# Four-layer graph network on one core: layer 1's own-feature half of the last 12 node tiles moved beside the stage's first gathers

## The chip, the cores and the metric

The kernel runs on one core of one Trainium2 chip. The metric is the device time of one execution in microseconds; of several executions the median is given. A core has a matrix engine (PE, with its weight loads listed apart as PEld), a vector engine (DVE), an activation engine (ACT), a general engine (POOL) and a queue engine for transfers (SP). Each executes its own list of instructions in order, and semaphores tie them together. SBUF is the working memory (128 partitions), PSUM holds the matrix engine's results in 8 banks. Transfers run on 16 DMA engines shared by all queues.

## The reference, cut to what matters

There are 6250 nodes with 256 features and 100000 edges sorted by their target `dst`, whose density falls towards high node numbers. Rows are normalised and rectified, and four graph layers follow; the result is added to x.

```python
def _sage_mean(h, src, dst, n, deg, W_self, W_neigh, b):
    msum = jax.ops.segment_sum(h[src], dst, num_segments=n)
    h_neigh = msum / jnp.clip(deg, 1.0)[:, None]
    return h @ W_self + h_neigh @ W_neigh + b
...
h = _sage_mean(features, edge_src, edge_dst, n, deg, W1_self, W1_neigh, b1)
h = _sage_pool(h, edge_src, edge_dst, n, deg, W2_pool, b2_pool, W2_self, W2_neigh, b2)
h = _sage_gcn(h, edge_src, edge_dst, n, deg, W3_neigh, b3)
h = _sage_mean(h, edge_src, edge_dst, n, deg, W4_self, W4_neigh, b4)
return h @ W_fc + b_fc
```

`_sage_pool` applies relu(h @ W_pool + b_pool) to every node before it takes the maximum over the sources of a node's edges. The change lies in layer 1, whose output is used only through products that the kernel has folded together: W1_self @ W2_pool (`Wa`), W1_neigh @ W2_pool (`Wb`) and one bias row (`crow`). So layer 1 computes for every node the row relu(h0 Wa + mean Wb + crow), where h0 are the node's own normalised features and mean is the mean over its sources.

## The kernel before, in words

The nodes are cut into 49 tiles of 128 (`NT` = 49). The first 8 (`H1`) are hub tiles with very many edges; their sums are computed as dense products with count matrices, which the kernel builds on the way. The other 41 are tail tiles, whose edges are gathered row by row.

A first stage, until about 105 us, normalises the rows. It keeps the result as three bf16 parts side by side in SBUF (`Z1`, 3 x 256 columns a tile, whose sum is the fp32 value), writes the same to the table `tab_h`, and computes `Wa`, `Wb` and `crow`.

Layer 1's main loop is the helper `sums` (lines 460 to 543). It runs over 474 steps, one for every 128 edges of the tail. In each step POOL gathers 128 source rows into one of 14 slots of `ring` (L483), DVE makes a one-hot matrix of the targets (L479), and PE multiplies it with the three parts of the rows (L505) into a PSUM bank. After four steps DVE adds that bank into the accumulators of the tiles that it touches (L532, L534). Each step then advances three lists of side work: the hub's builds and dense products (L337 to L351 and L564), spread evenly over all but the last 24 steps; `todo`, the tiles that are being finished, at most two at a time; and `aside`, a list of generators of which the first is advanced by one `yield` a step until it is exhausted, then the next. Before, `aside` holds `tail_checks` (small tests of the sorted order on DVE) and `segments` (loads and small DVE work for layer 2). What is left in `aside` and `todo` after the last step is run off behind it.

A tile is finished by the generator `done1` (lines 1094 to 1132): degree and scale on DVE, the mean `m1` on ACT (L1103); then, three steps later, PE turns the tile's own features (L1111: six bf16 products with the identity, three parts for each of two halves, which sum the parts in PSUM) and its mean (L1114) into the bank `pt`; ACT copies both halves into `th` (L1116), which SP stores in `tab_t` for layer 2 (L1117). Four steps later PE multiplies the own half with `Wa` (L1124, four instructions since a 512-column fp32 product with 128 rows appears as two) and, a step after that, the mean's half with `Wb` (L1127) into the bank `pm`. DVE adds `crow` (L1130), ACT rectifies (L1131), SP stores the row tile in `tab_p` (L1132, shown as rows). The pools `pst1` and `psm1`, which hold `pt` and `pm`, have one bank each, so two tiles can't hold them at once. Tail tiles finish in the order of their numbers, hub tiles between them as their dense products end.

Layer 2 begins with gathers from `tab_p` (L1475), which may touch any row, so the first of them needs the row stores of all tiles.

The order on each engine is set at build time by the framework: an instruction whose inputs are ready by its estimate can be placed before one that stands earlier in the program. DVE's order in the first stage is fixed by hand. Semaphores are placed by the framework.

Of the kernel before, what the change touches and what calls it, by code (L numbers as in the profile page):

```python
# [9 lines left out]
F32 = mybir.dt.float32  # L10
# [10 lines left out]
P = 128  # L21
# [56 lines left out]
def fast_path(  # L78
# [15 lines left out]
    nc = tc.nc  # L94
    N, FI = x.shape
    E = src.shape[0]
    FH = W1_self.shape[1]
    FO = W_fc.shape[1]
    NT = (N + P - 1) // P
# [5 lines left out]
    KI = FI // P  # L105
# [42 lines left out]
    for w0, w1_ in ((0, NW1), (NW1, NW)):  # L148
        for k in range(k_of[w0]):
            n = sum(1 for w in range(w0, w1_) if k_of[w] > k)  # L150
# [12 lines left out]
    tab_t = dram.tile([NT, P, FH], F32, name="tab_t")  # L163
# [42 lines left out]
    ident_b = const.tile([P, P], BF16, name="ident_b")  # L206
# [41 lines left out]
    def bank(pool, tag, name, shape=None, bufs=None):  # L248
        t = pool.tile([P, FH], F32, tag=one_tag.get(id(pool), tag), name=name, **({"bufs": bufs} if bufs else {}))
        if shape is None:  # L250
            return t
        n = math.prod(shape)
        if len(shape) == 1:
            return t[:, :n]
        return t[:, :n].rearrange("p (a b) -> p a b", b=shape[1])
# [340 lines left out]
    def segments():  # L596
        dstI, dstF, eqf = scratch(T, I32), scratch(T), scratch(T)
        flen, fhalf = (ahead.tile([P, 1], F32, name=n) for n in ("flenf", "fhalf"))
        flenI = ahead.tile([P, 1], I32, name="flenI")
        for b, tb in enumerate(BLOCKS):  # L600
            t0 = offs[b] // P
            for flat, put in ((sflat, srcI), (dflat, dstI)):
                tc.keep_in_program_order(nc.sync.dma_start(
                    put[:, t0 : t0 + tb],
                    flat[offs[b] : offs[b + 1]].rearrange("(p t) -> p t", t=tb),
                ))
        for _ in range(60):
            yield 1
        nc.vector.tensor_copy(dstF, dstI)
        nc.vector.tensor_tensor(same[:, 1:], dstF[:, 1:], dstF[:, : T - 1], op=ALU.is_equal)  # L610
        yield 1
        for b, tb in enumerate(BLOCKS):
            t0 = offs[b] // P
            sl_ = slice(t0, t0 + tb)
            nc.vector.memset(same[:, t0 : t0 + 1], 0.0)
            nc.vector.tensor_copy(rows_df[:, b : b + 1], dstF[:, t0 : t0 + 1])
            nc.vector.tensor_copy(rows_dl[:, b : b + 1], dstF[:, t0 + tb - 1 : t0 + tb])
            nc.vector.tensor_scalar(eqf[:, sl_], dstF[:, sl_], rows_df[:, b : b + 1], None,
                                    op0=ALU.is_equal)
            nc.vector.tensor_reduce(flen, eqf[:, sl_], AX.X, ALU.add)  # L620
            nc.vector.tensor_scalar(flen, flen, -1.0, None, op0=ALU.add)
            kept_row(b, flen, flenI, fhalf)
            nc.vector.tensor_scalar(flen, flen, float(P), float(run_at[b]), op0=ALU.mult,
                                    op1=ALU.add)
            nc.vector.tensor_add(fixI[:, b : b + 1], flen, pidx)
            yield 1
# [4 lines left out]
    Z1 = zpool.tile([P, NT, 3 * FI + 4], BF16, name="Z1")  # L631
# [6 lines left out]
    Wa = w1pool.tile([P, KI, FH], F32, name="Wa")  # L638
    Wb = w1pool.tile([P, KI, FH], F32, name="Wb")
    crow = w1pool.tile([P, FH], F32, name="crow")  # L640
# [12 lines left out]
    with ExitStack() as pro:  # L653
        pst = pro.enter_context(tc.tile_pool(name="pst0", bufs=3, space=PSUM))
# [299 lines left out]
        def tail_checks(pool):  # L954
            wrong = pool.tile([P, JR, P], BF16, name="wrongf", bufs=1)
            for c in range(JR):
                nc.vector.tensor_tensor(wrong[:, c, :], rD[:, c, :], rN[:, c, :], op=ALU.is_gt)
                yield 1
            nc.vector.tensor_reduce(bad[:, 0:1], wrong, AX.XY, ALU.max)
            yield 1  # L960
            far = wrong[:, : JR - JC, :]
            for c in range(JR - JC):
                nc.vector.tensor_tensor(
                    far[:, c, :].rearrange("p (g k) -> p g k", k=G),
                    d3[:, c, :].rearrange("p (g k) -> p g k", k=G),
                    dB[:, c * P // G : (c + 1) * P // G, None].to_broadcast([P, P // G, G]),
                    op=ALU.subtract,
                )
                yield 1
            nc.vector.tensor_scalar(dT, dT, float(NP), None, op0=ALU.is_lt)  # L970
            yield 1
            lo = g_of[H1][0] * G - JC * P
            for c in range(JR - JC):
                nc.vector.scalar_tensor_tensor(far[:, c, :], far[:, c, :], float(P), d3[:, c, :],
                                               op0=ALU.is_ge, op1=ALU.mult)
                yield 1
            nc.vector.tensor_reduce(bad[:, 2:3], far.rearrange("p c e -> p (c e)")[:, lo:],
                                    AX.X, ALU.max)
            yield 1
# [104 lines left out]
    with ExitStack() as on:  # L1084
        pst = on.enter_context(tc.tile_pool(name="pst1", bufs=1, space=PSUM))
        psm = on.enter_context(tc.tile_pool(name="psm1", bufs=1, space=PSUM))
        psg = on.enter_context(tc.tile_pool(name="psg1", bufs=2, space=PSUM))
        psd = on.enter_context(tc.tile_pool(name="psd1", bufs=2, space=PSUM))
        wk = on.enter_context(tc.tile_pool(name="fl1", bufs=2))

        def h0_row(s):
            return Z1[:, s, :]

        def done1(d, acc):
            r = rmean[:, d : d + 1]
            nc.vector.tensor_copy(deg[:, d : d + 1], acc[:, FI : FI + 1])
            nc.vector.tensor_scalar_max(r, acc[:, FI : FI + 1], 1.0)
            nc.vector.reciprocal(r, r)
            o = only[:, d : d + 1]
            nc.vector.tensor_scalar(o, acc[:, FI + 1 : FI + 2], float(P), None, op0=ALU.mult)  # L1100
            nc.vector.tensor_add(o, o, acc[:, FI + 2 : FI + 3])
            m1 = wk.tile([P, FI], F32, name="m1")
            nc.scalar.activation(m1, acc[:, :FI], AF.Copy, scale=r)  # L1103
            yield 1
            yield 1
            yield 1
            pt = bank(pst, "pt", "pt_m", (2 * KI, P))
            for k in range(KI):
                for part in range(3):
                    c = part * FI + k * P  # L1110
                    nc.tensor.matmul(pt[:, k, :], Z1[:, d, c : c + P], ident_b,  # L1111
                                     start=(part == 0), stop=(part == 2))
            for k in range(KI):
                nc.tensor.transpose(pt[:, KI + k, :], m1[:, k * P : (k + 1) * P], ident)  # L1114
            th = wk.tile([P, 2 * KI, P], F32, name="th")
            nc.scalar.copy(th, pt)  # L1116
            nc.sync.dma_start(tab_t[d].rearrange("p (k n) -> p k n", n=P), th)  # L1117
            yield 1
            yield 1
            yield 1  # L1120
            yield 1
            ph = bank(psm, "pm", "pm_hp")
            for k in range(KI):
                nc.tensor.matmul(ph, th[:, k, :], Wa[:, k, :], start=(k == 0), stop=False)  # L1124
            yield 1
            for k in range(KI):
                nc.tensor.matmul(ph, th[:, KI + k, :], Wb[:, k, :], start=False,  # L1127
                                 stop=(k == KI - 1))
            hp = wk.tile([P, FH], F32, name="hpf")
            nc.vector.tensor_add(hp, ph, crow)  # L1130
            nc.scalar.activation(hp, hp, AF.Relu)  # L1131
            nc.sync.dma_start(tab_p[d * P : (d + 1) * P, :], hp)  # L1132

        todo = []
        As.append(wk.tile([P, NT, P], F8, name="A1", bufs=1))
        builds = [None] + [build(d, As[d % 2], (sk1, mk1, 0), bpool, psb1) for d in range(1, H1)]
        denses = [dense(range(NT), lambda s, A=As[d % 2]: A[:, s, :], h0_row, FI, psd,
                        lambda acc, d=d: todo.append(done1(d, acc)), extra=3)
                  for d in range(H1)]
        work = []  # L1140
        for d in range(H1):
            work += merged(denses[d], builds[d + 1]) if d + 1 < H1 else denses[d]
        hub = Hub(made.rest() + work)
        sums(wk, psg, tab_h, FI, srcT, keyT, JC * P, H1, done1, 14, hub, counts=3, todo=todo, rest=24,
             aside=[tail_checks(wk), segments()])
    layer1.close()


# [1166 lines left out]
```

## Time and profile before

| | us |
|---|---|
| median of 3 runs | 2751.69 |
| lowest, highest | 2750.1, 2760.69 |
| profiled execution, time | 2753.24 |
| profiled execution, span from first to last instruction | 2751.4 |

| engine | busy us in the span | share |
|---|---|---|
| PE (matrix products) | 2372.0 | 86% |
| PEld (weight loads, beside PE) | 1281.9 | 47% |
| DVE | 2071.6 | 75% |
| ACT | 906.2 | 33% |
| POOL | 1942.6 | 71% |

All times in the views are microseconds from the first instruction. Layer 1's gathers run from 104.9 to 712.7 us, layer 2's from 738.3 to 1833.9 us. A share over the whole span mixes stages with different limits, so the views below are taken stretch by stretch. A group's row names line, engine, operation, what is written and read, shape and count, then busy time and mean duration in ns, then the idle time of its engine right before it and what ended that. A matrix product's duration is its latency; in a dense run they overlap, and the step from one start to the next is shorter (the 128x512 fp32 products of L1124 last 592 ns each, and a block of four takes 1.72 us in the chain). The granted clock is the share of full speed that PE was allowed.

### The profile page before, as it was taken

How to read it: one execution, taken by the hardware profiler on the slowest of the kernel's cores; microseconds unless marked ns; L12 is line 12 of the kernel's file. 1: busy time of each engine (PE TensorE's matmuls, PEld its weight loads, DVE VectorE, ACT ScalarE, POOL GpSimd, SP SyncE). 2: the span in 40 equal slices, each digit the busy share in tenths (PEclk: the TensorE clock that was granted, in tenths of full speed). 3: DMA queues.
4: the chain of work that ended last, by engine and by line, in shares of the span. 5: the costliest groups of instructions: out<-in, count | busy, mean ns of one | idle time of the engine just before them, and what ended most of it. 6: DMA issues, size and time to landing. Idle time of an engine off the chain costs nothing.

```text
span 2751.4 us, 39155 instructions
## 1 busy us (share of the span) xinstructions
PE 2372.0 (86%) x11540; PEld 1281.9 (47%) x11671; DVE 2071.6 (75%) x5542; ACT 906.2 (33%) x2177; POOL 1942.6 (71%) x2267
## 2 busy tenths in 40 slices
PE   3578999999887666798899969976999999999998
PEld 2245666776553322343344424432444444565554
DVE  8888777765599898789889988862667776466665
ACT  5467777763278786321311111110000101000000
POOL 6477777776467776777777777744777776677775
PEclk9799999999898787899999989998999999999999
DMA  9566777777699999999999999978999998888886
GB/s 286 154 170 192 208 211 217 229 220 211 207 362 356 328 360 340 364 352 350 327 358 356 359 340 340 343 251 313 373 380 389 387 368 303 259 239 241 240 243 198
DMA packets 350747, 806.43 MB, mean 293 GB/s; under 512 B 56014, under 2 KB 147638, under 8 KB 350492
## 3 DMA queue, kind: packets, MB, share of 16 engines
q0 software_dynamic: 146160, 514.05, 56.8%
q1 hardware_dynamic: 137784, 207.04, 20.7%
q10 hardware_dynamic: 66580, 82.73, 9.0%
q8 instruction: 94, 1.54, 0.2%
q14 instruction: 129, 1.06, 0.1%
HBM read 605.25 MB, written 199.17 MB: 292 GB/s over the span
## 4 chain that ended last, share of the span: by engine, by line
PE 32%; DMA 27%; DVE 8%; issue 5%; POOL 3%; ACT 0%; ACTq 0%; SPq 0%; DVEq 0%; POOLq 0%
DMA X<-rows,srcIf 12%; PE pd L564 11%; PE pg L505 6%; PE pd L556 4%; DMA rows<-X 3%; DVE run L1456 3%; DMA ring<-tab_r,srcE 3%; DMA ring<-tab_s,srcE 3%; DVE X L1456 2%; PE pd L557 2%; POOL X L1475 2%; PE pg L500 2%; PE pm_prf L1383 2%; DMA zt<-tab_r 2%; PE pm_prf L1377 1%
## 5 line engine op out<-in xcount | busy, mean ns | idle before, releaser
L1475 POOL DMA_INDIRECT X<-rows,srcIf x782 | 744.1, 952 | 276.4 <-issue 148.2
L1456 DVE SCALAR_TENSOR_TENSOR run<-run,samef,X 128x512 f32<-128x512 f32 x758 | 571.4, 754 | 45.3 <-DMA X<-rows,srcIf 41.4
L505 PE MATMUL pg<-ring,hot 128*128 128x259 bf16 (+1 forms) x2432 | 516.0, 322 | 68.4 <-DMA ring<-tab_h,srcT 39.5
L483 POOL DMA_INDIRECT ring<-tab_h,srcT x474 | 455.6, 961 | 157.6 <-issue 58.5
L534 DVE SCALAR_TENSOR_TENSOR acc<-pg,M,acc 128x256 f32<-128x256 f32 (+2 forms) x694 | 356.8, 539 | 116.0 <-PE pg L505 83.8
L483 POOL DMA_INDIRECT ring<-tab_r,srcE x342 | 333.7, 976 | 132.0 <-issue 59.4
L564 PE MATMUL pd<-r,ae 128*128 128x512 bf16 x1493 | 367.6, 384 | 37.2 <-DVE acc L1241 35.1
L483 POOL DMA_INDIRECT ring<-tab_s,srcE x314 | 299.8, 955 | 116.5 <-PE pg L501 35.2
L505 PEld LDWEIGHTS <-hot 128*128 128x128 bf16 x2448 | 240.3, 99 | 278.7 <-issue 120.1
L1456 DVE SCALAR_TENSOR_TENSOR X<-X,samef,run 128x512 f32<-128x512 f32 x379 | 281.4, 743 | 48.8 <-issue 17.8
L556 PE MATMUL pd<-zt,ac 128*128 128x512 bf16 x835 | 290.0, 380 | 7.4 <-DMA ac<-tab_a 5.8
L564 PEld LDWEIGHTS <-ae 128*128 128x128 fp8e4 x1536 | 151.2, 99 | 252.0 <-issue 107.0
L557 PE MATMUL pd<-zt,ac 128*128 128x256 bf16 x882 | 241.1, 273 | 2.7 <-DVE zt L312 0.2
L479 DVE TENSOR_SCALAR hot<-iota_bf,keyE 128x128 bf16<-128x128 bf16 x656 | 159.8, 268 | 106.6 <-PE pg L505 76.4
L564 PE MATMUL pd<-zt,ac 128*128 128x512 bf16 x797 | 221.2, 379 | 0.9
L1383 PE MATMUL pm_prf<-unf,hTf 128*128 128x512 f32 x392 | 191.3, 616 | 3.0 <-ACT hTf L1373 3.0
L338 ACT ACTIVATE hs<-ht,onef 128x128 bf16<-128x128 bf16 x396 | 153.8, 393 | 107.5 <-PE pb L346 106.4
L564 PE MATMUL pd<-Z,A 128*128 128x256 bf16 (+1 forms) x1176 | 184.3, 273 | 0.4 <-ACT A L351 0.3
L479 DVE TENSOR_SCALAR hot<-iota_bf,keyT 128x128 bf16<-128x128 bf16 x474 | 126.8, 276 | 53.8 <-PE pg L505 52.2
L346 PE MATMUL pb<-hm,hs 128*128 128x392 bf16 x461 | 147.9, 345 | 13.8 <-DVE hm L340 13.3
L337 ACT ACTIVATE ht<-iota_bf,sk 128x128 bf16<-128x128 bf16 x396 | 153.1, 398 | 8.4
L1391 ACT CAST r<-pm_prf 128x512 bf16<-128x512 f32 x49 | 28.7, 585 | 376.2 <-PE pm_prf L1383 303.3
(347 smaller groups left out, 3597.9 us busy)
## 6 DMA issues: line engine op xcount, KB each, us to landing
rows<-X SPq DMA_DIRECT2D x385, 256.0 KB
tab_r<-r ACTq DMA_DIRECT2D x49, 384.0 KB
tab_t<-th SPq DMA_DIRECT2D x49, 256.0 KB
rows<-hpf SPq DMA_DIRECT2D x49, 256.0 KB
th<-tab_t ACTq DMA_DIRECT2D x49, 256.0 KB
X<-rows,srcIf POOLq DMA_INDIRECT x782, 5.7
ac<-tab_a ACTq DMA_DIRECT2D x90, 112.0 KB
tab_h<-Z SPq DMA_DIRECT2D x16, 579.0 KB
```

What stands on the lines that cost most here:

```text
L337: nc.scalar.activation(t, iota_b, AF.Abs, bias=sk[:, r : r + 1])
L338: nc.scalar.activation(hots[0], t, AF.Relu, bias=one, scale=-1.0)
L479: nc.vector.tensor_scalar(hot[j], iota_b, keyT[:, j - jb : j - jb + 1], None, op0=ALU.is_equal)
L483: nc.gpsimd.indirect_dma_start(out=ring[:, j % deep, :], out_offset=None, in_=table, in_offset=bass.IndirectOffsetOnAxis(ap=srcT[:, j - jb ...
L505: nc.tensor.matmul(pg[:, : F + c], hot[j], X[:, part * F : (part + 1) * F + c], start=(k == 0 and part == 2), stop=(k == n - 1 and part == 1),
L534: nc.vector.scalar_tensor_tensor(acc[d], half, m, acc[d], op0=ALU.mult, op1=ALU.add)
L556: nc.tensor.matmul(hold[0], a, z[:, : 2 * F], start=(s == ss[0]), stop=False)
L557: nc.tensor.matmul(hold[0][:, :F], a, z[:, 2 * F :], start=False, stop=(s == ss[-1]))
L564: nc.tensor.matmul(hold[0][:, : F + c], a, z[:, part * F : (part + 1) * F + c], start=(s == ss[0] and part == 2 and s != own), stop=(s == ...
L1383: nc.tensor.matmul(pm, hT[:, c, :], un[:, c, :], start=False, stop=(c == KH - 1))
L1456: nc.vector.scalar_tensor_tensor(put, held, st, row, op0=ALU.mult, op1=ALU.max)
L1475: nc.gpsimd.indirect_dma_start(out=X[:, k, :], out_offset=None, in_=tab_p, in_offset=bass.IndirectOffsetOnAxis(ap=srcI[:, t : t + 1], axis=0),
```

## The change

A new generator, `own_ahead`, stands first in `aside`. For the tiles 37 to 48 (`AHEAD` = 49 - 12 to the end) it does the half of the finish that needs only the tile's own features: the six products with the identity, a copy to SBUF (`tho`, one buffer), the store of the first half of `tab_t[d]`, the product with `Wa`, and the addition of `crow` into a tile `own{d}` of its own, which stays in SBUF (12 x 2 KB a partition). It uses the same banks `pt` and `pm` as `done1`. It yields six times a tile. For those tiles `done1` leaves out the six products and the product with `Wa`, copies and stores only the second half, starts its product with `Wb` afresh, and adds `own{d}` where it added `crow`. The first 37 tiles are finished as before.

```diff
+        AHEAD = NT - 12
+        own1 = {}
+
+        def own_ahead():
+            for d in range(AHEAD, NT):
+                pt = bank(pst, "pt", "pt_o", (2 * KI, P))
+                for k in range(KI):
+                    for part in range(3):
+                        c = part * FI + k * P
+                        nc.tensor.matmul(pt[:, k, :], Z1[:, d, c : c + P], ident_b,
+                                         start=(part == 0), stop=(part == 2))
+                t = wk.tile([P, KI, P], F32, name="tho", bufs=1)
+                nc.scalar.copy(t, pt[:, :KI, :])
+                nc.sync.dma_start(tab_t[d][:, : KI * P].rearrange("p (k n) -> p k n", n=P), t)
+                yield 1
+                yield 1
+                ph = bank(psm, "pm", "pm_o")
+                for k in range(KI):
+                    nc.tensor.matmul(ph, t[:, k, :], Wa[:, k, :], start=(k == 0),
+                                     stop=(k == KI - 1))
+                    yield 1
+                own1[d] = wk.tile([P, FH], F32, name=f"own{d}", bufs=1)
+                nc.vector.tensor_add(own1[d], ph, crow)
+                yield 1
+                yield 1
+
         def done1(d, acc):
...
             pt = bank(pst, "pt", "pt_m", (2 * KI, P))
-            for k in range(KI):
-                for part in range(3):
-                    c = part * FI + k * P
-                    nc.tensor.matmul(pt[:, k, :], Z1[:, d, c : c + P], ident_b,
-                                     start=(part == 0), stop=(part == 2))
+            h0 = KI if d >= AHEAD else 0
+            if not h0:
+                for k in range(KI):
+                    for part in range(3):
+                        c = part * FI + k * P
+                        nc.tensor.matmul(pt[:, k, :], Z1[:, d, c : c + P], ident_b,
+                                         start=(part == 0), stop=(part == 2))
...
-            nc.scalar.copy(th, pt)
-            nc.sync.dma_start(tab_t[d].rearrange("p (k n) -> p k n", n=P), th)
+            nc.scalar.copy(th[:, h0:, :], pt[:, h0:, :])
+            nc.sync.dma_start(tab_t[d][:, h0 * P :].rearrange("p (k n) -> p k n", n=P),
+                              th[:, h0:, :])
...
-            for k in range(KI):
-                nc.tensor.matmul(ph, th[:, k, :], Wa[:, k, :], start=(k == 0), stop=False)
+            if not h0:
+                for k in range(KI):
+                    nc.tensor.matmul(ph, th[:, k, :], Wa[:, k, :], start=(k == 0), stop=False)
...
-                nc.tensor.matmul(ph, th[:, KI + k, :], Wb[:, k, :], start=False,
+                nc.tensor.matmul(ph, th[:, KI + k, :], Wb[:, k, :], start=bool(h0 and k == 0),
                                  stop=(k == KI - 1))
...
-            nc.vector.tensor_add(hp, ph, crow)
+            nc.vector.tensor_add(hp, ph, own1[d] if h0 else crow)
...
         sums(wk, psg, tab_h, FI, srcT, keyT, JC * P, H1, done1, 14, hub, counts=3, todo=todo, rest=24,
-             aside=[tail_checks(wk), segments()])
+             aside=[own_ahead(), tail_checks(wk), segments()])
```

## The prediction

> **What bounds the kernel now.** The change touches layer 1 alone, so I read the engines' busy time by stretch first. Columns: stretch, its length, then busy us and instruction count of PE, PEld, DVE, ACT, POOL, then granted clock, DMA share, GB/s.
>
> ```profile
> 105.00:200.00 95.00, 69.93 (x362) 40.19 (x363) 79.82 (x367) 51.93 (x138) 73.06 (x73) 0.83 0.62 172
> 200.00:300.00 100.00, 86.50 (x570) 58.09 (x569) 74.93 (x343) 71.38 (x207) 75.93 (x80) 0.98 0.69 202
> 300.00:450.00 150.00, 145.11 (x1016) 103.39 (x1016) 112.41 (x419) 111.64 (x304) 113.74 (x120) 1.00 0.71 209
> 450.00:600.00 150.00, 150.00 (x1028) 105.64 (x1026) 110.19 (x406) 103.58 (x277) 113.44 (x121) 1.00 0.74 218
> 600.00:720.00 120.00, 119.89 (x809) 83.00 (x807) 67.08 (x260) 46.76 (x107) 79.38 (x84) 1.00 0.70 210
> ```
>
> PE has slack early (25.1 us idle up to 200, 13.5 us up to 300) and none from 450 on. POOL does about 120 instructions per 150 us, one per 1.25 us, from 200 to 600, then only 84 in 120 us. So I looked at the 474 gathers of L483 over the whole stage, then in two stretches, the second with what ended POOL's idle time there.
>
> ```profile
> L483 POOL DMA_INDIRECT ring<-tab_h,srcT x474: 941/947/1407, 104.9 to 712.7; - x158
> DMA to landing us min/median/max: 3.0/3.5/6.3
> ...
> L483 POOL DMA_INDIRECT ring<-tab_h,srcT x177: 942/947/1061, 400.0 to 621.1; - x177
> ...
> L483 POOL DMA_INDIRECT ring<-tab_h,srcT x66: 941/946/1014, 622.3 to 712.7; - x66
> ...
>   PE pg L505: 15.3, 21
> ```
>
> Between 400.0 and 621.1, 177 gathers have 176 steps of 1.256 us: that is POOL's own pace (947 ns each, the rest the gap before the next). Between 622.3 and 712.7 the 65 steps take 90.4 us; at 1.254 us they would take 81.5. **8.9 us are lost**, and PE's L505 ended 15.3 us of the idle: a gather overwrites the ring slot of 14 gathers before, and PE is late in freeing it. Before 600 POOL sets the pace, after it PE does. What PE does there, in the stretch 616 to 735, by group (busy, mean ns, idle before):
>
> ```profile
> L505 PE MATMUL pg<-ring,hot 128*128 128x256 bf16 (+1 forms) x246 | 38.0, 273 | 0.0
> L564 PE MATMUL pd<-Z,A 128*128 128x256 bf16 (+1 forms) x255 | 36.7, 273 | 0.1
> L1127 PE MATMUL pm_hp<-Wb,th 128*128 128x512 f32 x59 | 27.8, 592 | 0.0
> L1124 PE MATMUL pm_hp<-Wa,th 128*128 128x512 f32 x56 | 26.6, 597 | 0.9 <-ACT th L1116 0.7 <-DVE hpf L1130 0.2
> L1111 PE MATMUL pt_m<-ident_b,Z 128*128 128x128 bf16 x84 | 7.0, 219 | 0.0
> ```
>
> The last view is the chain that ended last, here from the last ring product to layer 2's first gather (start us, length, what), with two earlier pieces for the price of one tile, and one row of L505 for when the ring products end:
>
> ```profile
> 663.99 1.72 PE pm_hp L1124 x4
> 665.71 0.34 PE pt_m L1111 x6
> ...
> 724.64 0.70 DVE hpf L1130
> 725.38 1.98 PE pm_hp L1124 x4
> 727.37 1.72 PE pm_hp L1127 x4
> 729.38 0.59 ACT th L1116
> 730.02 1.98 PE pm_hp L1124 x4
> 732.00 1.73 PE pm_hp L1127 x4
> 733.82 0.70 DVE hpf L1130
> 734.54 0.64 ACT hpf L1131
> 735.20 2.01 DMA rows<-hpf
> 737.85 0.41 issue
> 738.26 1.07 POOL X L1475
> ```
>
> ```profile
> L505 PE MATMUL pg<-ring,hot x234: 271/273/275, 622.4 to 724.6; 128*128 128x256 bf16 x78, 128*128 128x259 bf16 x39
> ```
>
> The last gather starts at 712.7, but its products end only at 724.6, 11.9 us later, where a landing of 3.5 us would allow about 5: PE carries some 7 us of backlog. Then the last two tiles run one behind the other through the single bank pm, and layer 2's first gather follows the last row store by about a microsecond. Layer 2 starts when layer 1 ends, so time won here is won in the whole.
>
> **The change, part by part.** *Removed from the late part.* Which tiles fall there is told by the ACT rows of L1103, which begin a tile's finish:
>
> ```profile
> L1103 ACT ACTIVATE m<-acc,rmeanf x12: 492/508/509, 609.6 to 726.5; 128x256 f32<-128x256 f32 x12
> ```
>
> Twelve tail tiles begin their finish from 609.6 on: exactly tiles 37 to 48. Each loses six L1111 (0.34 us) and four L1124 (1.72 us) on PE, 2.06 us by the two chain pieces; twelve are **24.7 us**, all from a stretch where PE has under 3 us idle. (The groups hold 14 tiles, 56 and 84 instructions: two are hub tiles, which keep theirs.) The copy L1116 is halved; DVE's L1130 stays.
>
> What that is worth has a floor, POOL's pace. Less PE work of 24.7 us against a backlog and loss of 7 + 8.9 = 16 us means PE is no longer the limit: the 65 steps run at 1.254 us and the last gather starts at 622.3 + 81.5 = 703.8. PE can follow: from 622 to 724.6 it is busy all 102.3 us; ten of the removed tiles' work, 20.6 us, lies in it (the Wa of the last two lies behind, the first transposes before); 102.3 - 20.6 = 81.7 us of work against 81.5 us of gathers. It is just enough, and the two or three microseconds by which it might not be are eaten by the slack of the last 24 gathers, in which the hub has ended. The last products then end about 5 us after the last gather (3.5 landing, 0.95 issue, six products), at 708.8 instead of 724.6: **15.8 us**.
>
> *The tail.* From 724.64 to 738.26 are 13.6 us. Two L1124 blocks of 1.98 us go, and half the copy of 0.59 us. The nearest row for a half copy is this one, 0.37 us:
>
> ```profile
> L276 ACT COPY B4f<-pm_w x8: 372/372/377, 752.9 to 779.5; 128x256 f32<-128x256 f32 x8
> ```
>
> 13.6 - 3.96 - 0.2 = 9.4 us: **4.2 us** less. For tile 48 alone acc, m1, transposes, copy and one L1127 block come to the same, so no other wait takes its place. Sum of gains: 15.8 + 4.2 = 20.0 us.
>
> *Added early.* own_ahead advances one step per gather, six steps a tile, so 72 gathers or 90 us: 105 to about 195. Per tile six transposing products, a half copy on ACT, a store on SP, four Wa products, and one DVE add of 128x512 as in L1130 (0.70 us in the chain). PE gets 24.7 us at full clock; the early Wa blocks are slower, and PE's waits there are these (105 to 200):
>
> ```profile
> L505 PE MATMUL pg<-ring,hot 128*128 128x256 bf16 (+1 forms) x210 | 44.8, 312 | 25.1 <-DMA ring<-tab_h,srcT 22.1 <-DVE acc L534 1.3 <-DVE hm L340 0.9
> ...
> L1124 PE MATMUL pm_hp<-Wa,th 128*128 128x512 f32 x8 | 4.9, 696 | 0.0
> ...
> L338 ACT ACTIVATE hs<-ht,onef 128x128 bf16<-128x128 bf16 x60 | 23.5, 393 | 21.9 <-PE pb L346 21.7
> ```
>
> At 696/592 the price is 29 us, against 25.1 us idle, of which 22.1 wait for gathers that POOL hasn't brought: the cover. What is left, 4 us, makes PE late but not POOL: 14 slots less the three in flight are 11 gathers or 13.8 us of reserve, and 200 to 300 has 13.5 us idle to win it back. If the cover were gone, all 29 us would count, since POOL has no slack anywhere. DVE gets 8.4 us and has 15.2 us free in 95; tail_checks, which stood first, moves behind. ACT gets 4.5 us, with 43 us free. SP gets twelve more stores; behind them wait the loads of srcI and the hub's stores, needed only after layer 1. The new wait is PE's Wa block on the ACT copy; behind it stand L505 and L346, and then POOL by way of the ring, DVE by way of acc.
>
> POOL already loses early: 73 instructions in 95 us are 3 short of 76, 3.8 us. I take as much again for the added traffic, 3.5 us; bounds are -4 us (PE busier at a higher clock, that loss gone) and +29.
>
> The Trainium skill, "TensorE: Matmul & The Clock Gate", Part 1, says that the PE clock halves after an idle window of about 3.4 us and returns after as much sustained work. The granted 0.83 early against 1.00 late agrees. By it the filled gaps would lift the clock for the old products too, and the early loss would be nil: 3.5 us better than my sum.
>
> **Sum.** 20.0 - 3.5 = 16.5 us. The profiled execution took 2753.24 us with a span of 2751.4; 2753.2 - 16.5 = 2736.7. The median of the runs, 2751.69, is 1.6 lower: **2735**.
>
> **The rivals.** *PE blocks early (slower).* Each Wa block waits on a copy that stands on ACT behind L338, which itself waits for PE: 21.7 us in 60 there. If that costs PE w per tile, POOL stalls by 29 + 12w - 25.1 - 13.8 us and the change loses once this passes 20: w = 2.5 us. At w = 4 us the stall is 38 us: 2751.7 + 38 - 20 = 2770. Against it: two gathers (2.5 us) lie between copy and product, and ACT is idle 45% of that stretch.
>
> *Only the tail wins.* If late PE busy hides waits for the gathers, removing work there frees nothing and only 4.2 us of the tail remain: 2747. Against: L505's idle there is 0.0, and the gathers wait for PE.
>
> *Given back in layer 2.* 25 KB more per partition stay held to the end of layer 1, and layer 2's first loads (bases of its constants and weights) are placed anew; if they come late by half the gain, 2743. For: layer 2's stretches are orders of waits too; against: its first gather waits for nothing but the row store.
>
> **Chances.** Forecast 0.62 (2729 to 2742), tail only 0.08, given back 0.19, blocked early 0.11. What a measurement can tell from no change is 0.5%, 13.8 us, thus 2738. Of the forecast 0.52 lies under that, with 0.02 of the third case: faster 0.54; blocked early gives slower 0.10; the rest, 0.36, within. The range runs from 2728 (early loss turned to a gain) to 2752, which takes in tail and given back and leaves out most of the blocked case.
>
> **What would show it.** Right: POOL's gather steps after 622 at 1.25 us, last start near 704 to 708, L505's last under 6 us after it, layer 2's first gather at 718 to 724; PE's idle up to 200 nearly gone, POOL's 73 instructions up to 200 down by three at most. Wrong: gather steps over 1.35 us between 105 and 300 with PE as releaser, Wa blocks of the new lines idle on ACT by over 2 us each, or layer 2's gathers taking longer than the 1095.6 us that they span now:
>
> ```profile
> L1475 POOL DMA_INDIRECT X<-rows,srcIf x782: 940/946/1437, 738.3 to 1833.9; - x196
> ```

## The result and the profile after

The changed kernel took 2730.28 us (median of five runs, 2726.8 to 2738.27); the kernel before, run beside it, 2751.52 (five runs, 2748.9 to 2760.69). The ratio is 0.9921, its 95% interval 0.99 to 0.9941: 16 to 28 us faster. The profiled execution took 2726.8 us with a span of 2725.0.

In the lines of the changed kernel the generator's products are L1112 (`Wa` times own features), its copy L1106 and its addition L1116; in `done1` the own transposes are L1139 (before L1111), the mean's L1142, the copy L1144, `Wa` L1154, `Wb` L1157, the addition of `crow` or `own` L1160 (before L1130), the activation L1161. Layer 2's gather is L1505. L483, L505, L534 and L564 have kept their numbers.

First the stretches of layer 1 after the change (stretch, length; busy us and count of PE, PEld, DVE, ACT, POOL; granted clock, DMA share, GB/s):

```profile
105.00:200.00 95.00, 81.09 (x469) 47.27 (x468) 80.28 (x347) 55.83 (x154) 72.44 (x75) 0.96 0.65 180
...
450.00:600.00 150.00, 150.00 (x1028) 105.51 (x1027) 108.63 (x405) 103.49 (x276) 113.61 (x119) 1.00 0.74 218
600.00:720.00 120.00, 110.32 (x732) 77.20 (x730) 69.49 (x280) 46.45 (x110) 78.82 (x83) 0.98 0.72 217
```

Early, PE's idle time went from 25.1 to 13.9 us and its clock from 0.83 to 0.96, while POOL issued 75 instructions instead of 73. Late, PE has 9.7 us idle where it had none. Next the gathers of the late part, with what ended POOL's idle time, then the rows of the ring products and of layer 2's gathers:

```profile
L483 POOL DMA_INDIRECT ring<-tab_h,srcT x67: 942/946/1051, 620.2 to 702.9; - x67
...
  PE pg L505: 6.4, 21
```

```profile
L505 PE MATMUL pg<-ring,hot x273: 270/273/417, 599.9 to 710.1; 128*128 128x256 bf16 x91, 128*128 128x259 bf16 x46
```

```profile
L1505 POOL DMA_INDIRECT X<-rows,srcIf x782: 940/946/1410, 720.7 to 1808.5; - x196
```

The 67 gathers have 66 steps in 82.7 us, 1.253 us each: POOL is at its own pace to the end. PE's L505 still stands as what ended 21 gaps, but these are 0.30 us each, the gap that POOL leaves between any two gathers at its own pace; before, 21 gaps took 15.3 us, and the 8.9 us above 21 times 0.305 are the loss. The last 66 begin one step after 620.2, at 621.45 (before 622.3), and end at 702.9 (before 712.7): 81.5 us for 65 steps instead of 90.4. The last ring product begins at 710.1 instead of 724.6, and layer 2 begins at 720.7 instead of 738.3, **17.6 us earlier**. What PE does between 616 and 720, by group (busy us, mean ns, idle before):

```profile
L505 PE MATMUL pg<-ring,hot 128*128 128x256 bf16 (+1 forms) x246 | 39.3, 274 | 4.8 <-DMA ring<-tab_h,srcT 3.8 <-DVE acc L534 0.9
L564 PE MATMUL pd<-Z,A 128*128 128x256 bf16 (+1 forms) x255 | 36.6, 273 | 0.0
L1157 PE MATMUL pm_hp<-Wb,th 128*128 128x512 f32 x57 | 27.8, 609 | 0.6 <-DVE hpf L1160 0.6
L1154 PE MATMUL pm_hp<-Wa,th 128*128 128x512 f32 x8 | 3.8, 601 | 0.0
L1139 PE MATMUL pt_m<-ident_b,Z 128*128 128x128 bf16 x12 | 1.0, 218 | 0.0
```

The products with `Wa` went from 56 to 8 and the own transposes from 84 to 12; 8 and 12 are the two hub tiles, which keep theirs. L505 now waits for gathers (3.8 us) where it waited for nothing: the roles of PE and POOL have changed places here. The chain that ended last, from the last gather on (start us, length, what):

```profile
701.70 4.53 DMA ring<-tab_h,srcT
...
706.36 0.59 PE pg L505 x2
706.95 0.43 PE pt_m L1142 x2
707.37 0.21 PE pg L505
707.59 2.50 PE pm_hp L1157 x4
...
710.17 0.70 DVE hpf L1160
...
711.01 1.95 PE pm_hp L1157 x4
...
713.69 0.43 PE rowsf L1298 x2
714.12 1.73 PE pm_hp L1157 x4
...
717.31 1.99 DMA rows<-hpf
...
720.71 1.02 POOL X L1505
```

From 710.1 to 720.7 are 10.6 us instead of 13.7: no `Wa` block is left in it. But a `Wb` block that took 1.72 us before takes 2.50 and 1.95 here. The 1.95 is no matter of the clock, which is 1.00 there: the block begins after a wait, as the `Wa` blocks of 1.98 us did before, and only a block right behind other products takes 1.72. For the 2.50, here are the timeline of PE ahead of it (start, length, what, idle time before it and what ended that) and two windows of the same execution (columns as above):

```profile
702.56 0.49 PE L505 MATMUL pg<-ring,hot 128*128 128x259 bf16 x3 [0.62 <-DMA ring<-tab_h,srcT]
704.22 0.49 PE L505 MATMUL pg<-ring,hot 128*128 128x259 bf16 x3 [1.17 <-DMA ring<-tab_h,srcT]
706.36 0.59 PE L505 MATMUL pg<-ring,hot 128*128 128x259 bf16 x2 [1.65 <-DMA ring<-tab_h,srcT]
```

```profile
702.20:705.60 3.40, 0.98 (x6) 0.48 (x5) 0.49 (x1) 0.05 (x1) 1.39 (x2) 1.00 0.91 261
705.60:709.00 3.40, 2.64 (x7) 1.59 (x8) 0.00 (x0) 0.37 (x1) 0.00 (x0) 0.50 0.20 58
```

PE waits for the last gathers, longer each time, and the granted clock is 0.50 from 705.6 to 709.0, where most of that block lies. The last ring products stand on PE behind it, so the last of them begins at 710.1, 7.2 us after the last gather began.

### The profile page after: what moved, and what is told of

It reads as the page before. It is cut to its first block, busy times and chain, and to the rows that moved or that the text cites. A ratio compares the mean times of both kernels' runs of the same rounds, so it can differ in the third digit from the quotient of the medians.

```text
span 2725.0 us, 39210 instructions
## 1 busy us (share of the span) xinstructions
PE 2361.1 (87%) x11540; PEld 1278.3 (47%) x11671; DVE 2080.1 (76%) x5554; ACT 905.1 (33%) x2189; POOL 1941.2 (71%) x2267
## 4 chain that ended last, share of the span: by engine, by line
PE 49%; DMA 29%; DVE 10%; issue 5%; POOL 3%; ACT 0%; SPq 0%; POOLq 0%; DVEq 0%; ACTq 0%
PE pd L564 13%; DMA X<-rows,srcIf 12%; PE pg L505 11%; PE pd L556 5%; DVE run L1486 4%; DMA ring<-tab_s,srcE 4%; DMA rows<-X 4%; DMA ring<-tab_h,srcT 4%; PE pm_hp L1157 3%; PE pd L557 3%; DVE X L1486 3%; PE pm_hp L1154 2%; POOL X L1505 2%; PE pb L346 2%; PE pg L500 2%
## 5 line engine op out<-in xcount | busy, mean ns | idle before, releaser
L1505 POOL DMA_INDIRECT X<-rows,srcIf x782 | 744.0, 951 | 269.2 <-issue 148.5
L483 POOL DMA_INDIRECT ring<-tab_h,srcT x474 | 455.6, 961 | 148.9 <-issue 51.8
L505 PE MATMUL pg<-ring,hot 128*128 128x259 bf16 (+1 forms) x2432 | 511.3, 319 | 56.8 <-DMA ring<-tab_h,srcT 33.5
L534 DVE SCALAR_TENSOR_TENSOR acc<-pg,M,acc 128x256 f32<-128x256 f32 (+2 forms) x694 | 356.2, 538 | 106.4 <-PE pg L505 82.4
L483 POOL DMA_INDIRECT ring<-tab_r,srcE x342 | 332.0, 971 | 131.9 <-issue 59.2
L564 PE MATMUL pd<-r,ae 128*128 128x512 bf16 x1493 | 367.8, 384 | 32.8 <-DVE acc L1271 30.5
L483 POOL DMA_INDIRECT ring<-tab_s,srcE x314 | 299.7, 955 | 117.0 <-PE pg L501 37.6
L505 PEld LDWEIGHTS <-hot 128*128 128x128 bf16 x2448 | 238.6, 98 | 262.2 <-issue 107.4
L564 PEld LDWEIGHTS <-ae 128*128 128x128 fp8e4 x1536 | 151.4, 99 | 249.3 <-issue 105.8
L564 PE MATMUL pd<-zt,ac 128*128 128x512 bf16 x797 | 221.3, 380 | 0.9
L564 PE MATMUL pd<-Z,A 128*128 128x256 bf16 (+1 forms) x1176 | 183.7, 273 | 0.8 <-ACT A L351 0.7
```

The source lines that it names most:

```text
L483: nc.gpsimd.indirect_dma_start(out=ring[:, j % deep, :], out_offset=None, in_=table, in_offset=bass.IndirectOffsetOnAxis(ap=srcT[:, j - jb ...
L505: nc.tensor.matmul(pg[:, : F + c], hot[j], X[:, part * F : (part + 1) * F + c], start=(k == 0 and part == 2), stop=(k == n - 1 and part == 1),
L534: nc.vector.scalar_tensor_tensor(acc[d], half, m, acc[d], op0=ALU.mult, op1=ALU.add)
L564: nc.tensor.matmul(hold[0][:, : F + c], a, z[:, part * F : (part + 1) * F + c], start=(s == ss[0] and part == 2 and s != own), stop=(s == ...
L1505: nc.gpsimd.indirect_dma_start(out=X[:, k, :], out_offset=None, in_=tab_p, in_offset=bass.IndirectOffsetOnAxis(ap=srcI[:, t : t + 1], axis=0),
```

## The experiments

The theory: late PE work held POOL up, and taking it away lets POOL run at its own pace and shortens the tail, while the same work early is covered by PE's waits for gathers. The rivals: only the tail wins; the early work costs as much as it saves elsewhere; the placement in layer 2's memory makes or takes the time. The measure is the start of layer 2's first gather, since runs of one kernel differ by several us in layer 2 itself. Each start comes from one traced execution; two such traces of the changed kernel on chips with the same times have 720.7 and 724.2, of the kernel before 738.3 and 739.6, so differences of 3 us or less decide nothing.

**The halves alone.** Three kernels and the changed kernel once more, on another chip of the same type. On that chip the kernel before takes 3247.17 us; what this means is told in the last section. The kernel before was not traced there, so the times of 720 to 742 us in these expectations, made for the first chip's pace, can't be compared one by one; what counts is how the four kernels stand to each other.

The changed kernel again:

> The changed kernel once more. If the 7.8 us by which layer 2's gathers were shorter in its first profile (1087.8 against 1095.6 us) belong to the change, they show again, and the time is 0.992 of before. If they were chance, the gathers take 1090 to 1100 us this time, and what stays is layer 1's gain: first gather of layer 2 at 720 to 722, time about 17.6 us less than before (0.9936).

The late half alone: the early work is gone, and `done1` does for the last 12 tiles only what it does in the changed kernel (the second half is stored twice, so that the bytes stay the same):

```diff
-             aside=[own_ahead(), tail_checks(wk), segments()])
+             aside=[tail_checks(wk), segments()])
...
-            nc.vector.tensor_add(hp, ph, own1[d] if h0 else crow)
+            nc.vector.tensor_add(hp, ph, crow)
...
+            if h0:
+                nc.sync.dma_start(tab_t[d][:, : h0 * P]..., th[:, h0:, :])
```

> The own-feature half of the last 12 tiles is left out altogether (nothing is computed early, the output lacks it). Theory one, the early work lies in PE's waits and costs nothing: layer 2's first gather at 720 to 721.5 as in the changed kernel, time within 2 us of it. Theory two, the early work costs the 3.5 us of my sum: first gather at 717, time 3.5 us under the changed kernel.

The early half alone: `own_ahead` runs, and `done1` is that of before, so the work of the 12 tiles is done twice.

> The early work is done, but each tile's finish is as before, so the 12 halves are computed twice. Theory one: layer 2's first gather at 737 to 739 as before, ratio to before 1.000. Theory two: 742, ratio 1.0013. If the early work blocks PE and stalls POOL, more than that, and the gathers of the first 100 us show steps over 1.35 us with PE as their releaser.

The early work moved into the middle of the gathers, where PE had next to no idle time in the first profiles:

```diff
         def own_ahead():
+            for _ in range(125):
+                yield 1
             for d in range(AHEAD, NT):
...
-             aside=[own_ahead(), tail_checks(wk), segments()])
+             aside=[tail_checks(wk), segments(), own_ahead()])
```

> The same work, but begun 219 gathers later (about 380 to 470 us), where PE is idle for 5 us in 150 only. Theory one, what counts is the idle time that covers it: 24.7 us of PE work find some 4 us of waits, PE runs late by 20 us, cannot win that back between 450 and 600, the ring's reserve of 14 us is used up and POOL stalls; layer 2's first gather at 728 to 735, gain over before 3 to 10 us. Rival, only the removal from the last 100 us counts: first gather at 720 to 722, time as the changed kernel.

| kernel | median us | ratio to before, 95% | last gather | last L505 | layer 2's first gather |
|---|---|---|---|---|---|
| changed, again | 3227.06 | 0.9936 [0.99, 0.9972] | 823.8 | 832.9 | 843.5 |
| late half alone | 3238.55 | 0.9976 [0.9946, 1.0005] | 821.8 | 833.9 | 844.5 |
| early half alone | 3239.98 | 0.9979 [0.9949, 1.0009] | 825.7 | 842.1 | 856.1 |
| early work in the middle | 3252.1 | 1.001 [0.998, 1.0041] | 835.8 | 844.2 | 854.8 |

The layer 2 gathers of the four, in this order (their span decides much of the time, and differs by up to 24 us between kernels with the same layer 2):

```profile
L1505 POOL DMA_INDIRECT X<-rows,srcIf x782: 940/946/1462, 843.5 to 2204.4; - x196
```

```profile
L1508 POOL DMA_INDIRECT X<-rows,srcIf x782: 940/946/1323, 844.5 to 2211.1; - x196
```

```profile
L1501 POOL DMA_INDIRECT X<-rows,srcIf x782: 940/946/1440, 856.1 to 2198.5; - x196
```

```profile
L1507 POOL DMA_INDIRECT X<-rows,srcIf x782: 940/946/1462, 854.8 to 2205.4; - x196
```

With and without the early work layer 2 begins at 843.5 and 844.5: the early work costs nothing that can be seen at the end, though the last gather comes 2.0 us earlier without it. By the medians the kernel without it is 11.5 us slower than the changed one, which neither theory said; its layer 2 starts only 1.0 us later, so most of this lies behind layer 1. Of the four only the changed kernel is clear of the kernel before by its time. Keeping the early work and doing the late work as well gives 856.1, so the removal late is worth 12.6 us there, less than the 17.6 of the first pair of profiles. Moved into the middle, the same work loses 11.3 us of these 12.6. Where it loses them is in the gathers between 392 and 560 us (its products run from 453 to 564); first the changed kernel, then the one with the work in the middle:

```profile
L483 POOL DMA_INDIRECT ring<-tab_h,srcT x113: 940/946/1050, 392.1 to 558.6; - x113
...
  PE pg L505: 16.2, 13
  PE pb L346: 13.6, 13
```

```profile
L483 POOL DMA_INDIRECT ring<-tab_h,srcT x104: 940/945/1027, 392.2 to 559.9; - x104
...
  PE pb L346: 25.2, 25
  PE pg L505: 22.1, 18
```

Nine gathers fewer, and 47.3 us of POOL's idle time ended by PE instead of 29.8. PE is not full there: it is busy 146.2 of 168 us in the first and 154.2 in the second, so its idle time took up only part of the added work. The same instructions cost nothing in one place and nearly all they save in another.

**Shorter waits for the last three tiles**, to see whether the steps that `done1` yields hold the tail, beside the work in the middle again, on another chip (before: 3277.66 us):

```diff
-            yield 1
-            yield 1
-            yield 1
+            late = d >= NT - 3
+            yield 1
+            if not late:
+                yield 1
+                yield 1
...
-            yield 1
+            if not h0:
+                yield 1
             for k in range(KI):
                 nc.tensor.matmul(ph, th[:, KI + k, :], Wb[:, k, :], ...
```

(The four steps behind the store become one in the same way.)

> The changed kernel, but the last three tiles are finished with one step of waiting where there were three and one where there were four, and own-half tiles do the Wb product a step earlier. In the changed kernel's trace the Wb product of tile 46 begins at 707.4 though its input is ready at 701.5 and PE waits for gathers in between, and the last ring products stand behind it. If the end of layer 1 is set by that order, layer 2's first gather comes 2 to 4 us earlier than in the changed kernel (717 to 719 where that one has 720.7); if it is set by the landing of the last gathers alone, it stays at 720 to 721.

> The own-feature work placed 219 gathers later, as in a4_in_middle, which ran on a chip whose gathers take about 1.5 us each and where PE is never full. On a chip with gathers of 1.25 us: theory one (the covering idle time counts) says gathers with steps over 1.35 us released by PE between 400 and 712, layer 2's first gather at 728 to 735; the rival (only the removal from the last 100 us counts) says 720 to 722.

The short waits gave 3267.06 us, ratio 0.9968 [0.9943, 0.9992]; layer 2's first gather began 20.7 us after the last of layer 1, against 19.7 in the changed kernel on the chip of the experiments above. Nothing there speaks for the wait steps as what holds the tail. The work in the middle: 0.9984 [0.9957, 1.0012], layer 2 at 858.2, against 847.0 in the short-wait kernel of the same chip. Both once more, on yet another chip (before: 3278.46 us):

> The shorter waits of the last three tiles once more, for a chip like that of d1_after, where the stretch from the last gather to layer 2's first took 18.6 us (17.8 in the first profile, 15.0 with nine tiles ahead, where the last ring products do not stand behind a Wb product). If the order on PE in that stretch costs these 3 us, it is 14 to 16 us here and the time 2 to 3 us under the changed kernel's ratio of 0.9935; if not, 17 to 19 us.

> The early work placed 219 gathers later once more, for a chip like that of d1_after. Theory one (the covering idle time counts): gather steps from number 216 to 384 longer than 1.26 us on the mean by 5 us or more in sum, layer 2's first gather at 728 to 735. Rival (only the removal from the last 100 us counts): 720 to 725 as in d1_after.

0.9983 [0.9956, 1.001], layer 2 at 858.7 (22.4 us after the last gather), and 1.0008 [0.998, 1.0036], layer 2 at 864.9. Both chips were again of the slower kind, so the bounds in these four expectations, made for gathers of 1.25 us, could not be met or missed. The work in the middle was run three times and showed no gain in any of them; on all three chips layer 2 began 6 to 11 us later than in a kernel with the work early, and 104 to 106 gathers began between 389 and 560 us where the other had 112 to 114. Whether shorter waits would help on the first chip's kind was not tried.

**How many tiles.** On a chip with the first one's times (before: 2753.91 us), the kernel before, the changed kernel, and six and nine tiles ahead instead of twelve:

```diff
-        AHEAD = NT - 12
+        AHEAD = NT - 6
```

> The kernel before, profiled beside the others of this call. If the chip is one of those on which PE loses time without a releaser (the time near 3250 us), layer 2's first gather comes at 855 to 858, as in the run that computes the halves twice, and PE, not POOL, sets the gathers' steps through most of layer 1; on a chip as in the first profile it comes at 738.

> The changed kernel beside it. Theory one: layer 2's first gather 12 to 18 us earlier than in d0_before; layer 2's gathers span the same in both within the spread of runs (difference under 8 us of either sign), so that layer 1 is all of the gain. If layer 2 gains by the change, its span is again 5 us or more shorter.

> Only the last 6 tiles are done ahead: 12.4 us of PE work moved in place of 24.7. Theory one, each tile's 2.06 us of PE is won one for one as long as PE sets the pace, and both tail blocks are among the six: layer 2's first gather 7 to 10 us later than in d1_after on a chip where PE sets the pace to the end, 5 to 8 us later on the first chip, where POOL's pace is reached with eight tiles. Rival, all of the gain is the tail's: as d1_after.

> The last 9 tiles ahead: 18.5 us of PE work. Theory one: on the first chip within 2 us of d1_after, since POOL's pace is the floor; on a chip where PE sets the pace 4 to 6 us later than d1_after, half way between it and b1_six.

The late gathers of the four, with POOL's waits for PE, and their layer 2 rows, in the order before, twelve, six, nine:

```profile
L483 POOL DMA_INDIRECT ring<-tab_h,srcT x68: 940/946/992, 620.8 to 713.9; - x68
...
  PE pg L505: 16.1, 22
```

```profile
L483 POOL DMA_INDIRECT ring<-tab_h,srcT x69: 942/946/1041, 620.3 to 705.6; - x69
...
  PE pg L505: 6.1, 20
```

```profile
L483 POOL DMA_INDIRECT ring<-tab_h,srcT x69: 940/946/997, 620.8 to 714.7; - x69
...
  PE pg L505: 13.6, 19
```

```profile
L483 POOL DMA_INDIRECT ring<-tab_h,srcT x68: 940/946/1005, 620.8 to 706.4; - x68
...
  PE pg L505: 7.7, 20
```

```profile
L1475 POOL DMA_INDIRECT X<-rows,srcIf x782: 940/946/1583, 739.6 to 1833.7; - x196
```

```profile
L1505 POOL DMA_INDIRECT X<-rows,srcIf x782: 940/946/1421, 724.2 to 1817.4; - x196
```

```profile
L1505 POOL DMA_INDIRECT X<-rows,srcIf x782: 940/946/1412, 731.5 to 1823.9; - x196
```

```profile
L1505 POOL DMA_INDIRECT X<-rows,srcIf x782: 940/946/1403, 721.4 to 1819.4; - x196
```

| tiles ahead | median us | ratio to before, 95% | layer 2's first gather | layer 2's gathers, span |
|---|---|---|---|---|
| none | 2755.34 | 1.0011 [0.9998, 1.0023] | 739.6 | 1094.1 |
| six | 2744.48 | 0.9967 [0.9951, 0.9983] | 731.5 | 1092.4 |
| nine | 2739.03 | 0.994 [0.9917, 0.9963] | 721.4 | 1098.0 |
| twelve | 2735.61 | 0.9935 [0.9916, 0.9954] | 724.2 | 1093.2 |

The gain of the change repeats: 19.7 us in the medians, 15.4 at the start of layer 2. Six tiles lose 7.3 us of it, nine none. That agrees with POOL's floor: the prediction had 16 us of loss and backlog to remove at 2.06 us a tile; six tiles remove 12.4 us, too little, nine remove 18.5, enough. With six, PE still ends 13.6 us of POOL's idle time, with nine and twelve 7.7 and 6.1. But the tiles don't count one for one: with six, the 68 steps take 93.9 us, 8.7 over 1.253 us a step, where the kernel before loses 9.1 in 67. Its gain of 8.1 us lies behind the last gather, in less backlog and a shorter tail: its gathers lose their last steps before 693 us, and the first of its six tiles begins its finish only at 688.3. Nine against twelve isn't decided: layer 2 begins 2.8 us earlier with nine, against 2 at most as expected, the medians stand the other way, and the intervals cover each other. In these two traces most of the difference is PE's clock. In both kernels the last ring products stand right behind a `Wb` block (the expectation for the short waits, which says otherwise of nine, misread this); it takes 3.43 us with twelve, while with nine PE runs through it without a wait and the step to the next product is 1.72 us, at a granted clock of 1.00. PE was busier with nine just before; whether that kept the clock up wasn't tested. The block with twelve (in the chain) and with nine (in PE's timeline, with the ring products behind it), then the stretch 700 to 720, twelve and nine:

```profile
710.09 3.43 PE pm_hp L1157 x4
```

```profile
709.29 1.88 PE L1157 MATMUL pm_hp<-Wb,th 128*128 128x512 f32 x4
711.01 0.49 PE L505 MATMUL pg<-ring,hot 128*128 128x259 bf16 x3
```

```profile
700.00:720.00 20.00, 15.46 (x58) 7.91 (x58) 5.81 (x25) 4.42 (x9) 5.06 (x6) 0.83 0.50 146
```

```profile
700.00:720.00 20.00, 16.18 (x78) 9.05 (x76) 7.97 (x30) 6.06 (x12) 5.67 (x6) 1.00 0.63 219
```

## Why the prediction was right, point by point

Forecast 2735 us, range 2728 to 2752, measured 2730.28 us: direction and mechanism as forecast, the gain somewhat larger. In layer 1 the terms were 15.8 + 4.2 - 3.5 = 16.5 us; the first pair of profiles has 14.5 + 3.1 + 0 = 17.6. That the sum comes so close is partly luck: the two gains were 2.4 us too large and the price 3.5 us too dear. The other 4 us or so of the median's 21 lie within the interval.

- **The late part: right, and the term a little too large.** The 65 gather steps took 81.5 us, as worked out, and 8.9 us came back. Six and nine tiles show that POOL's pace is the floor. The step that was off is "about 5 us after the last gather": it was 7.2. Its sum counts the issue twice, for a landing is counted from the gather's start (the chain's 701.70 row begins with its gather), so its own terms give about 4. Two things were not in it: the last gather but one took 4.5 us to land instead of 3.5, and the `Wb` block of 2.50 us, partly at half clock, ran on PE before the last ring products. Forecast 15.8, measured 14.5, of which 0.85 is the lead that the gathers already had at 621.
- **The tail: right in kind, 1.1 us too large.** The blocks of `Wa` went, but the first place after a wait, which makes a block longer (1.98 us for `Wa` before), passed to a `Wb` block: it took 1.95 us in the chain instead of 1.72, at a granted clock of 1.00. Two small products of L1298 (0.43 us) now stand between the last copy and the last `Wb` block, and from the end of the last row store to the first gather pass 1.4 us instead of 1.1. Forecast 4.2, measured 3.1.
- **The early price: mis-sized, 3.5 us forecast, none measured.** The step was "as much again for the added traffic", for which no row was given. POOL issued two more instructions up to 200, not three fewer, and gather steps were 0.85 us ahead at 621; in the repeated pair the same gather came 0.8 us later than before. On the chip of the four kernels POOL issued 61 and 64 instructions up to 200 us with the early work, 65 and 64 without. Running the late half without the early work gave 844.5 against 843.5 at layer 2's start, and a price of up to some 3 us would be lost in the spread of the traces. PE's part of it was too dear as well: half of the added products took 592 ns or less, and the 41 between 105 and 200 us took 630 on the mean, not 696. So one sign did not come: PE's idle time up to 200 was to be nearly gone, and 13.9 of 25.1 us stayed, since the old products became shorter too (L505 280 ns on the mean instead of 312). The row of L1112 (from the view of the copy `tho`, up to 205 us; durations are min, median and max in ns; the last line is what PE's products and their weight loads waited for, us and times):

```profile
L1112 PE MATMUL pm_o<-Wa,tho x48: 590/592/1219, 101.1 to 202.3; 128*128 128x512 f32 x48
...
  ACT tho L1106: 2.6, 2
```

 The rule weighed in the prediction, that of the Trainium skill, "TensorE: Matmul & The Clock Gate", Part 1, had the early loss at nil. It came out at nil, and the clock rose from 0.83 to 0.96. The added work does raise the clock: in the repeated pair it went from 0.85 to 0.94, and on the chip of the four kernels it was 0.80 and 0.82 with the early work and 0.74 in both without. That this is why the price was nil isn't shown: in the repeated pair POOL issued 73 instructions both times. And the idle window of the rule is not what this trace has: before the change the clock was 0.50 in five stretches of 3.4 us between 127 and 189 us, while no idle time of PE between 120 and 189 us was longer than 2.51 us. The agreement that the prediction saw is one of direction alone.
- **PE blocked early: refuted.** The rival needed 2.5 us of waiting per tile on the copy; that last line has two waits of 2.6 us in all for twelve tiles. Where PE did hold POOL up, with the same work in the middle, the gain was lost.
- **Only the tail wins: refuted** by the 8.9 us of gather steps.
- **Given back in layer 2: not seen.** Its gathers span 1095.6 us before and 1087.8 after in the first profiles, which would be 7.8 us won; the repeated pair has 1094.1 and 1093.2, and nine tiles, with less memory held than twelve, 1098.0. The instructions of DVE, POOL and SP in layer 2 stand in the same order in both kernels. The 7.8 us did not come again. Holding the memory without the change was not tried.

## What to carry to other kernels

Look for the stretch in which the engine that others wait for has no idle time and for one in which it waits itself: moving work from the first to the second is worth the lost steps of the engine that it held up, with the backlog and the tail that go with it, and no more than brings that engine back to its own pace (nine tiles did what twelve did). The place it goes to decides: the same work over 200 gathers later, where POOL already waited for PE, gave nearly all of it back on the slower chips. When the floor is another engine's pace, the freed engine waits before the tail, so price the tail's products above their dense duration: here the first block after a wait took 1.95 to 1.98 us instead of 1.72, and at half clock up to 3.43.

## What the runs showed of the hardware

Not every chip ran this kernel alike. Where the first profiles and those with six and nine tiles were taken, the kernel before needs 2752 to 2755 us; on three other chips it needs 3247, 3278 and 3278. The same changed kernel on the first of these three, in a stretch that PE filled completely above (1028 products, POOL 119 instructions):

```profile
450.00:600.00 150.00, 131.64 (x847) 88.67 (x846) 92.83 (x347) 93.80 (x245) 93.96 (x99) 0.97 0.62 180
```

PE does 847 products in the same time at nearly the same clock. Of its idle time there, 18 us, the trace gives ACT as what ended 11.3 us and nothing for 6.9, where above PE had no wait at all. The cause stays open. On that chip PE holds POOL up through most of layer 1: from 105 to 820 us it ends 136 us of POOL's idle time in 125 waits, which at POOL's own gap of 0.3 us would be 38. That may be why the early and middle placements differ so clearly there; on the first kind of chip the middle placement was not tried.

The clock fell in the tail without a long pause. In the 3.4 us before 705.6, PE was busy for 0.98 us in short pieces, with no idle time over 1.2 us, and the next 3.4 us had a clock of 0.50. The same holds for the changed kernel's second trace (busy 1.66 of 3.4 us, then 6.8 us at 0.50) and for the five early stretches before the change, each of which follows 3.4 us in which PE was busy 26 to 52%. No run looked for the share at which the clock falls. The Trainium skill, "TensorE: Matmul & The Clock Gate", section "A second HAM failure mode: psum-queue depth-cycling", tells of another kernel whose clock swings because PE idles briefly and often while it cycles through PSUM banks; here the short waits are for gathers, and the clock swings too.

Early gathers of layer 1 now and then last longer than 0.95 us. The row up to 205 us after the change, with the longest at 1237 ns (before 1407 over the whole stage):

```profile
L483 POOL DMA_INDIRECT ring<-tab_h,srcT x79: 942/947/1237, 104.2 to 204.6; - x79
```

The length is the gather's own, not a wait ahead of it. What the gathers up to 200 us take above 947 ns each comes to 4.1 us before and 2.8 us after, about POOL's early shortfall before the change (3.8 us); what lengthens them wasn't found.
